# Softmax denominators as three bfloat16 parts, spread back by one bfloat16 matmul two steps later

## The chip, the cores and the metric

The kernel runs on one core of one Trainium2 chip, as one program. The core has a matrix engine (PE, whose weight loads the profile keeps apart as PEld), a vector engine (DVE), a scalar engine (ACT), GpSimd (POOL) and a sync engine (SP) that issues most of the transfers. Each engine takes its instructions in the order in which they were written; engines wait for one another and for transfers by semaphores. The metric is the time of one execution on the device in microseconds, lower is better.

## The reference

A post-norm transformer layer on 8 sequences of 1024 tokens, width 256, in float32. Only the attention matters here:

```
scores = einsum('bhid,bhjd->bhij', q, k) * scale + gated_bias
attn   = softmax(scores, axis=-1)
out    = einsum('bhij,bhjd->bhid', attn, v)         # 16 heads of 16
x      = layernorm(x + out @ Wo.T + bo)
x      = layernorm(x + moe(x))                      # 8 experts, top 2, with a capacity
```

The bias of a pair of positions depends on their distance and on a gate of the query. The softmax is computed as exponentials, whose sums over the keys come out of the same product as the numerators; the division by these sums is the part that is changed.

## The kernel before, in words

The attention comes first (about the first 2570 us of the trace), then the experts. The attention is cut into 64 **units**: a unit is two heads of one sequence, a **batch** of eight units is one sequence. A unit is 16 **steps** of the main loop (L1296): step s handles key block j = s // 2 and query half c = s % 2. In a step, PE makes the scores of two heads (L1093), DVE adds the gated bias near the diagonal (L1108), ACT takes the exponential (L1115), and at odd steps PE multiplies the last exponentials with the values (L1123), which are extended by a column of ones, so that rows 0 to 15 of each group of 32 in `o_acc` are numerators and row 16 is their sum. Beside this each step finds the row maxima of a unit 21 steps ahead: two half products on PE (L1009, L1013), a relu on ACT (L1038), a fold on DVE (L1050). POOL makes the gated bias `gb` for a key block four steps ahead, once in two steps (L969), and a diagonal of gates `dgb`, once in two steps (L982).

The order is written out by hand: the loop issues the instructions, each engine runs its own in that order. Around the fixed work of a step hang **streams**, Python generators that advance by what they yield: the prologue of the next batch (projections, `pq`, `pv`, `pg`, `pgt`), the epilogue of the last one (output projection `po`, norm, router: `px`, `pl`, `pc`), and sixteen scatters of its rows, which are indirect transfers that POOL issues one at an odd step (L874). They share one PSUM bank, `bank`; a stream that holds it lets no other in (L1222), and generators in `own` (`divide`, `shift`) go ahead of the rest. `after(n, f)` runs f in the n-th following call of `free`, once in a step (L1212, L443).

What is done with a unit u's sums runs in the steps of unit u+1:

- at the end of step 1 ACT copies `o_acc` to `osb` (`take_outputs`, L1132, copy L1135);
- at step 2 SP issues four transfers that spread the four rows of sums over 128 partitions, 16 numbers each (`move_sums`, L1140);
- at step 4 DVE takes the reciprocals of this 128x16 tile (L1156);
- at step 5 SP issues four transfers that bring them back as four rows of 512, `recs` (`move_back`, L1150);
- at step 8 (`DIVIDE_AT`) PE multiplies a 4x128 selector with `recs` in float32, which puts each row on its group of 32 partitions (`divide`, L1163); at step 9 DVE multiplies `osb` by it (L1167) and SP stores the four outputs into `oD` (L1177).

SP's queue in those steps also has the loads of unit u+3: `ks` at step 3, `ks_d` at step 4 (six transfers each), `qs` at step 6 (seven, L893 and L901); `bias` at step 8 (L936), `gates` at steps 9 and 15 (L951), `biasb` at step 1 (L915); the streams' stores (`gd`, `fd`, `kd`, `qd`, `dd`); zero fills once in four steps up to unit 22 (L397); and at step 13 the two stores of the next unit's shifts, `row` (L1078). These shifts are made by `shift` (L1061) from step 11 on (`SHIFT_AT`), and the scores of the next unit read them from its step 0 on. The step before step 11 lets no stream take the bank. Streams of a batch are started at step 12 of its first unit.

## Time and profile before

| | us |
|---|---|
| three runs | 3739.71, 3731.26, 3739.18; median 3739.18 |
| the profiled execution | 3731.06, of which its span 3729.3 |
| PE busy | 3300.4 (88%) |
| POOL busy | 2225.9 (60%), 1760.73 of the 2340 us from 200 to 2540, in the attention |
| ACT, DVE busy | 2039.4 (55%), 1905.9 (51%) |
| the matmul that spreads the reciprocals (L1163) | 78.8 busy, 72.4 idle before it |

Times in the profile are of this one execution. "L12" is a line of the kernel; `pb<-recs,sel` names what is written and what is read. In a timeline a row is a start, a duration, an engine, a line, an operation, and in brackets how long the engine sat idle before it and what ended that. Matmuls are pipelined: a row's duration is longer than the distance to the next row, and the distance is what a matmul costs in a row of them. The granted clock of PE (PEclk) is a share of its full rate.

### The profile page before, as it was taken

How to read it: one execution, taken by the hardware profiler on the slowest of the kernel's cores; microseconds unless marked ns; L12 is line 12 of the kernel's file. 1: busy time of each engine (PE TensorE's matmuls, PEld its weight loads, DVE VectorE, ACT ScalarE, POOL GpSimd, SP SyncE). 2: the span in 40 equal slices, each digit the busy share in tenths (PEclk: the TensorE clock that was granted, in tenths of full speed). 3: DMA queues.
4: the chain of work that ended last, by engine and by line, in shares of the span. 5: the costliest groups of instructions: out<-in, count | busy, mean ns of one | idle time of the engine just before them, and what ended most of it. 6: DMA issues, size and time to landing. Idle time of an engine off the chain costs nothing. (4 is left out here: it accounts for less than half of the span.)

```text
span 3729.3 us, 53473 instructions
## 1 busy us (share of the span) xinstructions
PE 3300.4 (88%) x16263; PEld 1659.6 (45%) x16263; DVE 1905.9 (51%) x5559; ACT 2039.4 (55%) x3084; POOL 2225.9 (60%) x2619
## 2 busy tenths in 40 slices
PE   2699899999999999999999999995199999999998
PEld 1233243333334334333433333332176667677776
DVE  2356565555665666566566565662034344344343
ACT  1377676767777777777776777772022222222222
POOL 2467566776786787787687788683333333333332
PEclk9799899999999999999999999997599999999999
DMA  4467656665553443443444434330323321233220
GB/s 107 125 186 192 174 158 179 190 188 178 170 159 112 133 134 121 149 125 121 131 138 137 136 115 138 118 111 27 106 51 89 88 87 57 90 93 95 69 90 22
DMA packets 380594, 455.71 MB, mean 122 GB/s; under 512 B 87653, under 2 KB 285410, under 8 KB 380282
## 3 DMA queue, kind: packets, MB, share of 16 engines
q1 hardware_dynamic: 338602, 388.06, 35.3%
q0 software_dynamic: 19296, 43.38, 4.0%
q10 hardware_dynamic: 22384, 20.58, 1.9%
q8 instruction: 138, 2.26, 0.2%
q14 instruction: 174, 1.43, 0.1%
HBM read 315.16 MB, written 140.54 MB: 122 GB/s over the span
## 5 line engine op out<-in xcount | busy, mean ns | idle before, releaser
L1115 ACT ACTIVATE pr<-sc 128x1024 f32<-128x1024 f32 x1024 | 1046.2, 1022 | 296.3 <-DVE sc L1108 291.9
L1050 DVE CUSTOM_DVE_ANT_0 over<-pm,over 128x512 f32<-128x512 f32 x1024 | 704.0, 687 | 906.8 <-ACT over L1038 335.9
L969 POOL TENSOR_TENSOR gb<-bias,gates 128x1024 f32<-128x1024 f32 (+2 forms) x512 | 1071.1, 2092 | 144.9 <-DMA gates<-gd 67.0
L1038 ACT ACTIVATE over<-pm 128x512 f32<-128x512 f32 x1024 | 609.3, 595 | 357.1 <-PE pm L1013 344.3
L1093 PE MATMUL sc<-qs,ks 122*128 122x512 bf16 x2048 | 622.6, 385 | 25.9 <-ACT pr L1115 16.9
L1108 DVE TENSOR_TENSOR sc<-sc,gb 128x640 f32<-128x640 f32 (+3 forms) x768 | 599.9, 781 | 58.5 <-POOL gb L969 34.4
L1013 PE MATMUL pm<-biasb,dgb 128*128 128x320 bf16 (+2 forms) x2048 | 580.8, 284 | 17.4 <-POOL dgb L982 17.0
L1123 PE MATMUL o_acc<-pr,v 128*17 128x512 f32 x4096 | 556.9, 616 | 0.3 <-ACT pr L1115 0.3
L1458 PE MATMUL ph<-xsT,w 128*128 128x512 f32 (+1 forms) x1440 | 488.0, 497 | 13.0 <-ACT xsT L1398 13.0
L1473 PE MATMUL py<-w,hT 128*128 128x256 f32 x2208 | 485.0, 379 | 5.3 <-DVE ys L1480 5.3
L1473 PEld LDWEIGHTS py<-w,hT 128*128 128x128 f32 x2208 | 419.2, 190 | 74.0 <-issue 10.3
L1009 PE MATMUL pm<-ks,qs 120*128 120x512 bf16 x1024 | 397.8, 388 | 40.0 <-DVE mh L1050 13.8
L1009 PE MATMUL pm<-ks_d,qs 120*128 120x512 bf16 x1024 | 395.6, 386 | 31.3 <-ACT over L1038 22.4
L1009 PEld LDWEIGHTS <-qs 120*128 120x128 bf16 x2048 | 208.4, 102 | 462.4 <-issue 296.2
L1465 ACT ACTIVATE hT<-ph,b_sb 128x512 f32<-128x512 f32 (+1 forms) x360 | 211.6, 588 | 287.7 <-PE ph L1458 287.7
L1458 PEld LDWEIGHTS ph<-xsT,w 128*128 128x128 f32 x1440 | 270.4, 190 | 212.9 <-issue 167.0
L1398 ACT COPY xsT<-pt 128x512 f32<-128x512 f32 (+1 forms) x90 | 39.5, 489 | 567.1 <-PE pt L1395 567.1
L1013 PEld LDWEIGHTS <-dgb 128*128 128x128 bf16 x2048 | 201.9, 99 | 304.0 <-issue 174.0
L143 POOL TENSOR_TENSOR rs<-rstd,neghalf 128x1 f32<-128x1 f32 x138 | 78.6, 570 | 427.3 <-DVE rstd L141 426.6
L982 POOL TENSOR_TENSOR dgb<-anti,grev 128x256 bf16<-128x256 f32 x512 | 315.0, 616 | 5.0
L1093 PEld LDWEIGHTS <-ks 122*128 122x128 bf16 x2048 | 198.0, 100 | 210.1 <-issue 64.1
L1493 POOL DMA_INDIRECT out_dram<-o,dst_i x138 | 145.6, 1055 | 168.7 <-DVE o L145 65.8
(184 smaller groups left out, 2837.7 us busy)
## 6 DMA issues: line engine op xcount, KB each, us to landing
gates<-gd SPq DMA_DIRECT2D x64, 832.0 KB
biasb<-stripb SPq DMA_DIRECT2D x128, 288.0 KB
gates<-gd SPq DMA_DIRECT2D x64, 576.0 KB
bias<-blocks SPq DMA_DIRECT2D x64, 512.0 KB
xd<-zero SPq DMA_DIRECT2D x51, 522.0 KB
ks<-kd SPq DMA_DIRECT2D x384, 64.0 KB
qs<-qd SPq DMA_DIRECT2D x384, 64.0 KB
yd<-zero SPq DMA_DIRECT2D x40, 512.0 KB
```

The source lines that it names most:

```text
L969: nc.gpsimd.tensor_tensor(gb_[:, :, off : off + hi - lo], me.bias[:, :, off : off + hi - lo], gates[:, :, lo - at : hi - at], ALU.mult,)
L982: nc.gpsimd.tensor_tensor(dg, anti.unsqueeze(1).to_broadcast([P, HP, P]), batches[b].grev[:, i, hp * HP : (hp + 1) * HP] .unsqueeze(2) .to ...
L1009: nc.tensor.matmul(pm, QS[u % 3][:R_SHIFT, h, i * P : (i + 1) * P], keys, start=True, stop=False)
L1013: nc.tensor.matmul(pm[:, lo:hi, :], dgb[m - h][:, h, :], me.biasb[:, at : at + (hi - lo) * P].rearrange("p (j n) -> p j n", n=P)[:, :, :HALF],
L1038: nc.scalar.activation(me.over, pm, AF.Relu)
L1050: nc.vector.tensor_tensor_reduce(out=me.over, in0=me.rest, in1=me.over, scale=1.0, scalar=-3.0e38, op0=ALU.add, op1=ALU.max, accum_out=me. ...
L1093: nc.tensor.matmul(me.sc[:, h, :], ks[:, h, j * P : (j + 1) * P], qs[:, h, c * CH : (c + 1) * CH], start=True, stop=True,)
L1108: nc.vector.tensor_tensor(sc[:, :, lo - c * CH : hi - c * CH], sc[:, :, lo - c * CH : hi - c * CH], me.gb[j][:, :, off : off + hi - lo], A ...
L1115: nc.scalar.activation(pr, sc, AF.Exp)
L1123: nc.tensor.matmul(o_acc[r : r + D + 1, :], batches[b].v[:, j, hp * HP + h, :], prs[c][:, h, :], start=(j == 0), stop=(j == NI - 1),)
L1458: nc.tensor.matmul(ph[:, :size], w1_sb[:, k, f * P : (f + 1) * P], xsT[:, k, :size], start=(k == 0), stop=(k == NK - 1),)
L1473: nc.tensor.matmul(py, hT[:, f, t * P : (t + 1) * P], w2_sb[:, f, :], start=(f == 0), stop=(f == NF - 1),)
```

## The change

The three cuts are made on the spread tile, after the reciprocal: POOL copies the remaining value to bfloat16 and subtracts the copy, so that three bfloat16 numbers add up to the float32 one. `move_back` brings three times four rows, `recs` is 12 rows of 512 in bfloat16, and the selector is 12x128 in bfloat16, one matmul that also adds the three parts. The cut is at step 5, `move_back` at step 6, the `qs` load at step 7 in place of 6, `divide` at step 10 in place of 8, and the streams of a batch start at step 14 of its first unit in place of 12.

```diff
-DIVIDE_AT = 8
+DIVIDE_AT = 10
...
-        sel = cst.tile([4, 4, 32], F32, name="sel")
+        sel = cst.tile([12, 4, 32], BF16, name="sel")
         nc.gpsimd.memset(sel, 0.0)
-        nc.gpsimd.affine_select(
-            out=sel, in_=sel, compare_op=ALU.not_equal, fill=1.0, base=0,
-            pattern=[[-1, 4], [0, 32]], channel_multiplier=1,
-        )
+        for a in range(3):
+            nc.gpsimd.affine_select(
+                out=sel, in_=sel, compare_op=ALU.not_equal, fill=1.0, base=-4 * a,
+                pattern=[[-1, 4], [0, 32]], channel_multiplier=1,
+            )
...
+            def cut():
+                rest = me.sums
+                me.rp = rt.tile([P, 3, 4 * CH // P], BF16, tag="rp", name=f"rp{u}")
+                for a in range(3):
+                    nc.gpsimd.tensor_copy(me.rp[:, a, :], rest)
+                    if a < 2:
+                        nc.gpsimd.tensor_tensor(
+                            rest, rest, me.rp[:, a, :], ALU.subtract
+                        )
             def move_back():
-                me.recs = rt.tile([4, CH], F32, tag="recs", name=f"recs{u}")
+                me.recs = rt.tile([12, CH], BF16, tag="recs", name=f"recs{u}")
                 for r in range(4):
-                    nc.sync.dma_start(
-                        out=me.recs[r : r + 1, :].rearrange("o (p n) -> o p n", p=32),
-                        in_=me.sums[r * 32 : (r + 1) * 32, :],
-                    )
+                    for a in range(3):
+                        nc.sync.dma_start(
+                            out=me.recs[a * 4 + r : a * 4 + r + 1, :].rearrange(
+                                "o (p n) -> o p n", p=32
+                            ),
+                            in_=me.rp[r * 32 : (r + 1) * 32, a, :],
+                        )
             after(1, move_sums)
             after(3, lambda: nc.vector.reciprocal(me.sums, me.sums))
-            after(4, move_back)
+            after(4, cut)
+            after(5, move_back)
...
-                if sb == 12:
+                if sb == 14:
...
-                    for which, at_ in enumerate((3, 4, 6)):
+                    for which, at_ in enumerate((3, 4, 7)):
```

## The prediction

> **What bounds the kernel now.** I read the page's slices first: the attention is the stretch to 2570 us; there PE shows 9 tenths nearly throughout, POOL 6 to 8. Then the waits, most of all those of the changed matmul.
>
> ```profile
> PE   2699899999999999999999999995199999999998
> POOL 2467566776786787787687788683333333333332
> PEclk9799899999999999999999999997599999999999
> ...
> PE pb L1163 <- DMA recs<-sums: 65.7, 25, 8.3
> DVE sc L1108 <- POOL gb L969: 34.4, 34, 2.6
> ```
>
> PE sets the pace, and in 25 of 64 units it stands still until the reciprocals have come back. I call "round i" the time between the copy of unit i's `o_acc` (L1135) and the next one. The timelines of SP and PE in round 53, which begins at 2221.71, show why it waits:
>
> ```profile
> 2222.34 2.45 SPq L1140 DMA_DIRECT2D sums<-osb  x4
> 2224.88 2.85 SPq L901 DMA_DIRECT2D ks<-kd  x6
> 2227.78 2.75 SPq L901 DMA_DIRECT2D ks_d<-dd  x6
> 2230.63 2.90 SPq L1150 DMA_DIRECT2D recs<-sums  x4
> ...
> 2233.15 0.27 PE L1013 MATMUL pm<-biasb,dgb 128*128 128x256 bf16 x1
> 2234.81 1.09 PE L1163 MATMUL pb<-recs,sel 4*128 4x512 f32 x2 [1.39 <-DMA recs<-sums]
> 2235.84 0.39 PE L1009 MATMUL pm<-ks,qs 120*128 120x512 bf16 x1
> 2236.06 0.27 PE L1013 MATMUL pm<-biasb,dgb 128*128 128x256 bf16 x1
> ...
> 2237.17 1.91 PE L1123 MATMUL o_acc<-pr,v 128*17 128x512 f32 x8
> ```
>
> SP is busy without a gap from 0.63 to 11.8 us of the round; PE starts 1.28 us after its last `recs` issue (13.10 against 11.82). The issues of SP are the path, at 0.61 us each (the usual four in 2.44). And a wait costs more than itself: the values product at 2237.17 takes 1.91 us, elsewhere 1.05. The windows around it have the clock (after PEld, DVE, ACT, POOL comes PEclk):
>
> ```profile
> 2232.00:2236.00 4.00, 2.61 (x13) 0.91 (x10) 1.18 (x3) 2.69 (x4) 3.74 (x10) 1.00 0.19 58
> 2236.00:2240.00 4.00, 4.00 (x17) 0.98 (x16) 2.37 (x7) 1.62 (x2) 2.30 (x8) 0.60 0.72 216
> 2240.00:2244.00 4.00, 4.00 (x25) 1.61 (x24) 2.99 (x7) 2.76 (x4) 3.47 (x9) 0.98 0.44 163
> ```
>
> After 1.39 us of waiting the clock is 0.60 for 4 us. Of 20 waits of over 1.2 us in the rounds at places 4 to 7 of a batch, 19 are followed by such a slow product; scores to the next step's L1009 take 4.13 there for 2.61. I count 1.2 us a wait.
>
> POOL is the second thing to see, in round 30 (from 1354.07), where it also issues scatters:
>
> ```profile
> 1363.10 2.38 POOL L969 TENSOR_TENSOR gb<-bias,gates 128x1024 f32<-128x1024 f32 x1
> 1365.41 0.63 POOL L982 TENSOR_TENSOR dgb<-anti,grev 128x256 bf16<-128x256 f32 x1
> 1366.21 1.01 POOL L874 DMA_INDIRECT xd<-xt,slot_i  x1 [0.17 <-issue]
> 1367.25 2.36 POOL L969 TENSOR_TENSOR gb<-bias,gates 128x1024 f32<-128x1024 f32 x1
> 1369.54 0.33 POOL L929 MEMSET biasb<- 64x256 bf16 x1
> ...
> 1367.06 1.09 PE L1163 MATMUL pb<-recs,sel 4*128 4x512 f32 x2 [2.29 <-DMA recs<-sums]
> ```
>
> The memset is step 7's, so the `dgb` before it is step 5's: POOL reaches step 5 at 12.0 us of the round, PE had reached step 8 at 10.7. A pair of steps costs POOL 4.14 us with a scatter, PE 3.6. This lag is in all rounds at places 6 and 7 of batches 1 to 6 (10.0 to 15.9 us), nowhere else in the light rounds (4.0 to 7.3).
>
> **The change part by part.**
>
> *The matmul.* From its start to the next product it takes 1.03 us (2234.81 to 2235.84); a bf16 product over 512 columns steps in 0.22 (2235.84 to 2236.06). Saved 0.81 x 64 = 52 us, all on PE's path.
>
> *Eight more issues and two steps.* `recs` takes 12 x 0.61 = 7.3 us of SP. No trace has 32-byte pieces; bounds per issue are SP's cheapest here (0.42, `bias`) and 0.68, what `recs` costs between zero fills; I take 0.61, the same 32 pieces. The `qs` load stays behind `recs`, so it neither helps nor hurts. In round 53 the issues would run from 8.92 to 16.2, and land at 17.5. Step 8 was ready at 11.7; step 10 is two steps later, 15.3. So the wait is 2.2 instead of 1.4: the two steps buy 3.6 us, the issues cost 4.9.
> - Place 5: +0.75 each, in six batches +5.
> - Place 4: no wait in rounds 28, 36, 52. Walking the streams' yields with starts two steps later, `dd` and `qd` come to lie ahead of `recs` there (+1.1), landing 18.7 against 12.75 + 3.6 + 0.5 for one more count: 1.8 and 1.2 for the clock. Four batches +12, two with zero fills +5.
> - Batch 0: four waits of 4.8 instead of 3.55: +5.
> - Places 0, 2, 3: step 10 comes at 20 to 25 us, landing at 18 to 21: nothing. If streams were lighter there it would be 1 to 2 each.
>
> *The cut on POOL.* Five small operations. The nearest rows, 128x8 (0.19 to 0.21, 0.28 apart when dependent), give 1.3 us; at most 5 x 0.32 (128x64). Where POOL keeps up this lies beside SP's loads: in round 53 it would run from 6.0 to 7.3, SP comes at 8.9. Behind it on POOL wait the scatter and step 6's `gb`, needed four steps later. But at places 6 and 7 POOL is late, and now SP stands at `recs` behind it, with `qs`, `bias` and `gates` in the queue. Round 30: cut 12.0 to 13.3, issues to 20.6, landed 21.9, while step 10 was due at 14.3: a wait of 7.6. POOL works on through it and its next step 5, at 48.5 from the same start, becomes 49: cut to 50.4, landing 59.0, while PE, from 21.9 on, is there after 16 steps, the transpose and the clock (30.8), at 52.7: 6.3 more. Then 20.1 to the end of round 31, with `po` twice: 79.1 for the two rounds, where rounds 14/15, 22/23, ... 54/55 took 72.7, 69.0, 69.0, 72.3, 69.3, 70.1, mean 70.4. Without the saving already counted that is +10.3, six times: +62. Bounds: nothing, if POOL's catching up pays for it all, and +13, if the later wait is as the first.
>
> *The `row` store.* At place 1 of batches 0 to 6 SP has 18 `gd`/`fd` stores and no gap; `row` ends at 30.1 to 31.0 in rounds 25 to 49, lands 2.1 later (round 17), and the next scores start at 33.9. After: +4.9 for issues, +0.5 since POOL's cut ends at 10.3, -1.6 as `kd` and `dd` fall behind `row`: landing 36.5. PE has one projection less before it (-1.5): 32.4. A wait of 4.1 and 1.2: six rounds (round 1 has 5 us to spare) +30. Bounds: 0, if SP's stretch breaks up, and +50.
>
> *End.* In round 63 nothing covers the chain: sums, reciprocal, cut 1.3, eight issues 4.9: +6.3. Rounds 58 to 62 by the same sums: +9. The selector's two more selects, 0.3 each, lie in the setup beside loads; at worst +0.6. The stream's bank slot moves from step 10 to 8, as many as before; nothing.
>
> Sum: -52 +5 +17 +5 +62 +30 +15 = +82. Against the profiled 3731.06 that is 3813; the median of the runs is 8 higher, I add half of it: 3817.
>
> The Trainium skill, "TensorE: Matmul & The Clock Gate", section "Why this matters for your kernels", asks for no idle gaps of PE above about 3 us. The row above has the clock down after 1.39 us, so the measurement decides; by the rule the waits of 1.8 to 2.2 us would cost no clock, and the sum would be about 7 less (six waits of place 4 at 1.2). "DMA: Bandwidth & Descriptors", "Rules for kernel authors", says to gather many small transfers into a large one, as below 64 KB one pays mostly overhead; that speaks against twelve transfers of 1 KB in place of four of 2 KB, and the rows agree: 0.61 us an issue whatever it carries.
>
> **Rivals.**
> - *SP late, POOL not* (0.20): PE's stall in the first round of a pair is time that POOL owed anyway (DVE waits for `gb` there, 34.4 us in all). The +62 go, half of the 30 with the looser queue: 82 - 62 - 15 = +5 to +25, 3740 to 3765. Against it: those 34.4 us are all it could give back.
> - *Hidden, faster* (0.08): if an issue of 32-byte pieces took under 0.42 us, round 53's twelve would land by 15.2, in time for 15.3. Then 52 us are saved, and most of the 57 us of waits before the last round with some 20 clock drops: -50 to -100, 3640 to 3690. Against it: none of the 512 issues of such shape took less than 0.50.
> - *The matmul stays dear* (0.02): if three parts cost as much as two float32 passes, +52 on the sum, 3869. Every bf16 row speaks against it.
> - *The queue breaks down* (0.03): `row` late in more rounds, 3880 to 3920.
> - *They cancel* (0.05): within 0.3% of before, 11 us, which is about what this kernel's runs tell from nothing.
>
> **How the numbers follow.** The forecast (0.62) with the bounds of pair, row and issue gives 3775 to 3875. The range goes from 3746, which takes in most of the first rival, to 3875. Faster 0.08; same 0.09, with a fifth of the first rival; slower 0.83.
>
> **What would show it.** `pb` as one bf16 matmul x64 of about 0.4 us. `recs` x768, at about 0.6. PE's waits for `recs` well above 65.7 us, in over 30 units, the longest but the last at places 6 and 7, with SP idle before L1150 until POOL. More slices of PEclk below 9. PE's waits for `row` above 17 us. Wrong I would be if `recs` were issued faster, or if the lag of POOL at step 5 vanished with the streams' new places.

## The result and the profile after

The kernel after takes 3938.12 us in the median of four runs (3923.87 to 3943.97) and the kernel before 3739.09 (3731.26 to 3739.71). The ratio is 1.0531, with an interval of 1.0502 to 1.056: 199 us slower. The forecast was 78 us slower with a range up to 3875. The direction was right and the size was not.

The profiled execution of after has 3943.97 us, its span 3942.2. The experts take as long as before (2842.6 to 3942.2, before 2631.7 to 3729.3). What was added lies in the attention, from the first copy of `o_acc` on. These are the slices of the page (the span in 40 equal parts, tenths busy; PEclk is the granted clock):

```profile
PE   2678798878888988988998988887359999999998
...
POOL 2457566776776786787688677677223333333332
PEclk9889899989989989998998998889579999999999
```

PE had nines nearly throughout the attention; now most of its slices have an eight or less. PEclk is below nine in eleven slices before the end of the attention, where it was in two. POOL is not fuller per slice. PE stands still more often. The waits (engine, what it wanted to run, what ended the wait, then us in total, times, longest) say for what:

```profile
PE pb L1180 <- DMA recs<-rp: 134.8, 28, 13.8
...
PE pc L809 <- POOL incl L739: 79.0, 43, 7.7
PE pm L1011 <- DMA qs<-qd: 78.4, 35, 6.7
...
PE sc L1095 <- DMA qs<-row: 25.7, 7, 6.9
...
PE pm L1011 <- DVE mh L1052: 13.3, 35, 1.3
```

These are the same of the kernel before:

```profile
PE pc L807 <- POOL incl L737: 31.3, 17, 7.7
...
PE sc L1093 <- DMA qs<-row: 7.6, 4, 4.1
...
PE pm L1009 <- DMA qs<-qd: 5.0, 1, 5.0
```

The first has doubled (65.7 before, in 25 units). The third is new in the rounds: the one wait of 5.0 us before lies at 115 us, ahead of the first round, and after has one of 6.7 there and 34 in the rounds. It is the start of the row maxima of unit u+2 (u is the unit whose steps run), which reads the `qs` that SP has just loaded. The second is the epilogue's count of places. The loads of `gates` stand in the same queue: POOL waited 267.2 us for them, before 67.0, but DVE's wait for the `gb` that POOL makes from them is 29.1, before 34.4, so PE did not stand for that. Round 45, which begins at 2064.22, shows the new wait. First SP's queue, then PE:

```profile
2070.30 2.75 SPq L903 DMA_DIRECT2D ks_d<-dd  x6
2073.15 7.51 SPq L1164 DMA_DIRECT2D recs<-rp  x12
2080.70 0.55 SPq L895 DMA_DIRECT2D qs<-fd  x1
2081.30 2.85 SPq L903 DMA_DIRECT2D qs<-qd  x6
```

```profile
2081.87 0.37 PE L1180 MATMUL pb<-recs,sel 12*128 12x512 bf16 x1 [0.95 <-DVE sc L1110]
...
2086.05 0.61 PE L1011 MATMUL pm<-ks_d,qs 120*128 120x512 bf16 x1 [2.97 <-DMA qs<-qd]
...
2086.75 1.91 PE L1125 MATMUL o_acc<-pr,v 128*17 128x512 f32 x8
```

The twelve issues take 7.51 us. `recs` is there in time for `pb`, which is now one short bf16 matmul. But `qs` could be issued only behind it: its last issue ends at 2084.15, and PE, at step 11, waits 2.97 us until it has landed. The values product behind the wait takes 1.91 us and not 1.05. The windows (after PE, PEld, DVE, ACT and POOL comes PEclk) show the clock under it:

```profile
2078.00:2082.00 4.00, 3.05 (x19) 0.91 (x17) 2.79 (x9) 3.86 (x6) 3.84 (x9) 1.00 0.06 9
...
2086.00:2090.00 4.00, 3.95 (x15) 1.01 (x16) 0.31 (x1) 1.78 (x3) 1.52 (x3) 0.50 0.88 324
```

Of the values products of eight matmuls, 44 are now more than 0.3 us over the median of 1.05 (22 before), by 36.7 us together (17.0 before). These are called slow products below.

### The profile page after: what moved, and what is told of

Its sections match the earlier page's. It is cut to its first block, busy times and chain, and to the rows that moved or that the text cites. A ratio compares the mean times of both kernels' runs of the same rounds, so it can differ in the third digit from the quotient of the medians.

```text
span 3942.2 us, 54539 instructions
## 1 busy us (share of the span) xinstructions
PE 3317.5 (84%) x16199; PEld 1656.4 (42%) x16199; DVE 1909.4 (48%) x5559; ACT 2045.0 (52%) x3084; POOL 2285.4 (58%) x2941
## 3 DMA queue, kind: packets, MB, share of 16 engines
q8 instruction: 138, 2.26, 0.2%
## 5 line engine op out<-in xcount | busy, mean ns | idle before, releaser
L971 POOL TENSOR_TENSOR gb<-bias,gates 128x1024 f32<-128x1024 f32 (+2 forms) x512 | 1069.7, 2089 | 367.3 <-DMA gates<-gd 267.2
L1095 PE MATMUL sc<-qs,ks 122*128 122x512 bf16 x2048 | 640.7, 395 | 38.3 <-DMA qs<-row 25.7
L1015 PE MATMUL pm<-biasb,dgb 128*128 128x320 bf16 (+2 forms) x2048 | 590.2, 288 | 16.6 <-POOL dgb L984 16.6
L1125 PE MATMUL o_acc<-pr,v 128*17 128x512 f32 x4096 | 577.4, 636 | 0.3 <-ACT pr L1117 0.3
L1011 PE MATMUL pm<-ks_d,qs 120*128 120x512 bf16 x1024 | 404.2, 395 | 95.4 <-DMA qs<-qd 78.4
L1011 PE MATMUL pm<-ks,qs 120*128 120x512 bf16 x1024 | 410.3, 401 | 36.5 <-DVE mh L1052 13.3
```

The lines of the kernel that those rows point to most:

```text
L971: nc.gpsimd.tensor_tensor(gb_[:, :, off : off + hi - lo], me.bias[:, :, off : off + hi - lo], gates[:, :, lo - at : hi - at], ALU.mult,)
L1011: nc.tensor.matmul(pm, QS[u % 3][:R_SHIFT, h, i * P : (i + 1) * P], keys, start=True, stop=False)
L1015: nc.tensor.matmul(pm[:, lo:hi, :], dgb[m - h][:, h, :], me.biasb[:, at : at + (hi - lo) * P].rearrange("p (j n) -> p j n", n=P)[:, :, :HALF],
L1095: nc.tensor.matmul(me.sc[:, h, :], ks[:, h, j * P : (j + 1) * P], qs[:, h, c * CH : (c + 1) * CH], start=True, stop=True,)
L1125: nc.tensor.matmul(o_acc[r : r + D + 1, :], batches[b].v[:, j, hp * HP + h, :], prs[c][:, h, :], start=(j == 0), stop=(j == NI - 1),)
```

## The experiments

The theory after the result ("SP"): SP issues in order, `qs` stands behind `recs`, and the eight additional issues push it past step 11, where unit u+2's row maxima begin; the matmul's gain is real. The rivals: "POOL", the cut on POOL is what costs, by its time or by holding SP; and "places", the later divide and the later streams cost by themselves. The 95% interval is in brackets behind each ratio to the kernel before. 1% is 37.5 us. As before, place p means the rounds i with i mod 8 = p, here without round 62; sums over a place compare profiled executions. That of before has 3731.06 us, and the medians of before beside the experiments are 3746 to 3752, so, if that is spread evenly over the places, up to 2.6 us of such a sum is not the edit's.

**Eight more issues, and nothing else.** The kernel before, with

```diff
             def move_back():
...
+                spare = rt.tile([8, 32, 8], F32, tag="spare", name=f"spare{u}", bufs=1)
+                for r in range(8):
+                    nc.sync.dma_start(
+                        out=spare[r : r + 1, :, :],
+                        in_=me.sums[r % 4 * 32 : (r % 4 + 1) * 32, :8],
+                    )
```

> The kernel before, with eight more transfers of 32 pieces of 32 bytes issued by SP right behind recs, into a tile that nothing reads; matmul, divide step and cut are as before. Theory SP (SP's issues are in order, and eight more of them put the qs load past step 11, where unit u+2's row maxima begin): recs itself is as early as before, so the wait for recs stays near 65.7 us in 25 rounds, but qs lands 4.9 us later, about 21.4 us into a light round where step 11 is reached at 19.5; a wait for qs of about 1.9 us and 1.2 for the clock in some 30 rounds is 93, and about 4 for the row store in seven rounds is 28: near 3860, and the wait at pm for qs goes from 5.0 us to 50 or more. Theory POOL (the cut on POOL and the epilogue's later place on POOL are what costs): without them only the row store is late, 3740 to 3770. Theory places (the later divide and streams cost by themselves): 3740 to 3770 as well.

1.0429 [1.0406, 1.0451], 161 us more than before. The waits of this kernel:

```profile
PE pm L1009 <- DMA qs<-qd: 111.9, 38, 6.4
...
PE pb L1169 <- DMA recs<-sums: 63.9, 25, 8.3
...
PE sc L1093 <- DMA qs<-row: 27.4, 10, 5.2
```

The wait for `recs` is what it was (65.7), that for `qs` goes from 5.0 to 111.9, that for `row` from 7.6 to 27.4. Slow products go from 22 to 39. Round 37 of this kernel (from 1726.70) shows all of it, SP's issues and PE's two waits:

```profile
1735.63 2.54 SPq L1150 DMA_DIRECT2D recs<-sums  x4
1738.22 5.02 SPq L1156 DMA_DIRECT2D spare<-sums  x8
1743.29 0.55 SPq L893 DMA_DIRECT2D qs<-fd  x1
1743.88 2.67 SPq L901 DMA_DIRECT2D qs<-qd  x6
```

```profile
1739.46 1.09 PE L1169 MATMUL pb<-recs,sel 4*128 4x512 f32 x2 [1.05 <-DMA recs<-sums]
...
1748.89 0.58 PE L1009 MATMUL pm<-ks_d,qs 120*128 120x512 bf16 x1 [3.96 <-DMA qs<-qd]
```

`pb` waits 1.05 us (1.27 in the kernel before); nine us later the row maxima start after a wait of 3.96 for `qs`. Issues that nobody reads cost 161 us, 50 more than the theory gave: its 1.9 us a wait was too small (111.9 in 38 is 2.9).

**The moved places alone.** The kernel before, with

```diff
-DIVIDE_AT = 8
+DIVIDE_AT = 10
-            after(4, move_back)
+            after(5, move_back)
-                if sb == 12:
+                if sb == 14:
-                    for which, at_ in enumerate((3, 4, 6)):
+                    for which, at_ in enumerate((3, 4, 7)):
```

> The kernel before with the four moved places alone: divide at step 10, move_back at step 6, qs at step 7, the batch's streams from step 14. The matmul stays float32 with four transfers, and there is no cut. Theory SP: recs lands at 12.8 us of a light round and step 10 comes at 15.3, so of the 65.7 us at pb only the last round's 8 stay, with some 20 clock drops of 1.2: -80; qs is as early as before. 3655 to 3690. Theory POOL: the epilogue's later place brings back part, with PE's wait for incl at pc as in the changed kernel (79.0 us, before 31.3): 3690 to 3720. Theory places: that wait and the others take the whole gain, 3740 or more.

1.0013 [0.9994, 1.0033]. The wait for `recs` did fall, from 65.7 to 11.6 us, and none of it became time. By rounds of the profiled executions, places 5 and 6 are 25 us shorter in all, place 4 is 28 us longer and places 2 and 3 are 21 longer. These are the waits that took its place:

```profile
DVE sc L1108 <- POOL gb L969: 73.7, 49, 5.4
...
PE pc L807 <- POOL incl L737: 61.4, 35, 7.7
...
PE pm L1009 <- DMA qs<-qd: 21.6, 13, 6.8
```

They were 34.4, 31.3 and 5.0. So at place 7, where POOL is late (round 31 takes 37.5 us, before 35.7, with a wait of 3.80 for ACT in place of that for `recs`), PE's wait was time that POOL needed anyway, and the epilogue's counts at place 4 pay for the later streams. "Places" is right in that the move costs what it brings, and wrong in that it would explain the 199 us.

**Three parts in one transfer a row.** The kernel after, with `recs` as 4x32x3x16 and

```diff
-                    for a in range(3):
-                        nc.sync.dma_start(
-                            out=me.recs[a * 4 + r : a * 4 + r + 1, :]...
-                            in_=me.rp[r * 32 : (r + 1) * 32, a, :],
-                        )
+                    nc.sync.dma_start(
+                        out=me.recs[r : r + 1, :, :, :].rearrange("o p a n -> o p (a n)"),
+                        in_=me.rp[r * 32 : (r + 1) * 32, :, :].rearrange("p a n -> p (a n)"),
+                    )
...
+            for a in range(3):
+                nc.tensor.matmul(
+                    pb, sel.rearrange("p h m -> p (h m)"), me.recs[:, :, a, :],
+                    start=(a == 0), stop=(a == 2),
+                )
```

> The changed kernel, but the three parts of a row go in one transfer of 32 pieces of 96 bytes, so recs has four issues and not twelve; recs lies as four rows with the parts side by side, and pb is three accumulated bf16 matmuls of four rows in place of one of twelve (about 0.44 us more a unit, 28 in all). Cut on POOL and all places as in the changed kernel. Theory SP: the qs wait (78.4) goes and recs is in time except where POOL is late at places 6 and 7 and in the last round; against before -24 for the matmul, -60 for recs, -24 for the clock, +30 for the epilogue's wait for incl, +15 for POOL at places 6 and 7: 3660 to 3710. Theory POOL: most of the loss stays, over 3850. Theory places: 3800 or more.

1.0144 [1.0116, 1.0173], 3808.84 us: 145 less than after, though its matmul is dearer, but 100 over what "SP" gave. What was left was large, and its rounds say where: against the moved places alone, places 6 and 7 are 47 us longer (37.8 and 40.4 us in rounds 30 and 31; 31.2 and 37.5 with the moves alone), all others about as long or shorter.

**One part, at the old places.** The kernel before, with

```diff
-                me.recs = rt.tile([4, CH], F32, tag="recs", name=f"recs{u}")
+                me.recs = rt.tile([4, CH], BF16, tag="recs", name=f"recs{u}")
...
+            def turn():
+                me.rp = rt.tile([P, 4 * CH // P], BF16, tag="rp", name=f"rp{u}")
...
+                    nc.vector.reciprocal(me.rp, me.sums)
```

> The kernel before with recs in bfloat16, written so by DVE's reciprocal: the second and third parts are left out, so the reciprocals have eight bits. Four transfers of 32 pieces of 32 bytes, one bf16 matmul, all at the old places, no cut on POOL. What the matmul alone gives: 0.81 x 64 = 52 us less, 3680 to 3695, under all theories; if the wait for recs or something behind pb takes the gain, 3725 or more. The issues of 32-byte pieces at 0.61 us as those of 64 bytes; if they are cheaper, the wait of 65.7 us at pb is shorter.

0.9887 [0.9865, 0.9909], 43 us less. The bf16 matmul's gain is there when nothing else changes, somewhat under the 52 that a product's distance gave; the wait for `recs` is 60.2.

**The cut on DVE.** The kernel after, with

```diff
-                    nc.gpsimd.tensor_copy(me.rp[:, a, :], rest)
+                    nc.vector.tensor_copy(me.rp[:, a, :], rest)
                     if a < 2:
-                        nc.gpsimd.tensor_tensor(
+                        nc.vector.tensor_tensor(
```

> The changed kernel with the five operations of the cut on DVE in place of POOL, in the same step. So far: moved places alone +5 us, one part of bf16 at the old places -43, eight more issues alone +161, the changed kernel with four transfers in place of twelve +54 against before; what is left for the cut on POOL is about 5 - 24 + x = 54, so x = 73, of which places 6 and 7 of the batches hold 47 (37 and 40 us for the two rounds in place of 34 and 37 with the moved places alone). Theory both (issues and POOL each cost, and add up): 73 less than the changed kernel, a ratio of 1.030 to 1.040 to before; at places 6 and 7 SP no longer stands before recs, and PE's wait for incl at pc falls from 79.0 us to about 61 as with the moved places. Theory SP alone: under 10 us less, 1.050, since twelve issues keep PE waiting wherever the cut is made.

1.0563 [1.0535, 1.0592]: no gain at all. PE's wait for `recs` fell from 134.8 to 42.6 and that for the fold of the row maxima rose from 13.3 to 86.9. The cause is in DVE's own rows, here round 30 (from 1456.01):

```profile
1462.90 0.17 DVE L1154 CAST rp<-sums 128x16 bf16<-128x16 f32 x1
1463.11 0.17 DVE L1156 TENSOR_TENSOR sums<-sums,rp 128x16 f32<-128x16 f32 x1
1463.32 3.12 DVE L1154 CAST rp<-sums 128x16 bf16<-128x16 f32 x1
```

and in POOL's at the same time:

```profile
1462.99 1.01 POOL L876 DMA_INDIRECT xd<-xt,slot_i  x1 [0.17 <-issue]
1464.03 2.37 POOL L971 TENSOR_TENSOR gb<-bias,gates 128x1024 f32<-128x1024 f32 x1
```

The same cast of 16 numbers takes 0.17 us or 3.12: the long one ends at 1466.44, 0.04 after POOL's `gb` ends at 1466.40. Of the 320 operations of the cut 63 took over 1 us, and 51 of these end within 0.2 us of the end of a `gb`. So here a copy on DVE stood still while POOL worked on SBUF, and PE stood behind the fold behind it. What SP's shorter wait for POOL gave was paid back there.

**`ks_d` earlier.** The kernel after, with

```diff
-                    for which, at_ in enumerate((3, 4, 7)):
+                    for which, at_ in enumerate((3, 0, 7)):
```

> The changed kernel with one load moved: the six ks_d transfers of unit u+2 are issued at step 0 of unit u in place of step 4. Their buffer is free since step 11 of the unit before, and SP stands idle there in light rounds. Everything in the queue behind comes 2.75 us earlier: recs and qs. Theory qs (the deadline at step 11 is what the eight issues cost): in a light round qs lands at about 19.5 and PE is there at 20 or later, so the wait at pm for qs (78.4) falls under 25 and that for recs (134.8) to about 80, where POOL's cut is the later of the two; with 1.2 for the clock on some 30 rounds: 90 to 130 less than the changed kernel, a ratio of 1.018 to 1.030. Theory POOL alone: SP stands before recs until the cut is done, so only what is behind it in light rounds gains: under 40 less, 1.043 or more.

1.0367 [1.034, 1.0394], 61 us less than after, between what the two theories gave. The wait for `qs` fell only to 67.3: where `recs` came earlier PE did too, and `qs` still stood behind twelve issues; at places 6 and 7 and in round 28 SP stood at `recs` for POOL as before (round 28: `recs` issued from 11.2 to 18.7 us in both).

**All loads ahead, in the kernel before.** Only

```diff
-                    for which, at_ in enumerate((3, 4, 6)):
+                    for which, at_ in enumerate((1, 0, 3)):
```

> The kernel before with SP's order changed and nothing else: ks_d is loaded at step 0, ks at step 1 and qs at step 3, in place of 4, 3 and 6, so that recs stands behind sums and qs alone, and no load has to hurry behind it. If SP's issues alone made the wait of 65.7 us at pb, it falls to the last round's 8 and the clock gains 20 x 1.2: 3660 to 3680, 0.977 to 0.982. If POOL is the limit at places 6 and 7, as the moved places alone showed (the wait at pb gone there, 3.8 us for ACT behind DVE and gb in its place), 30 of it are given back there: 3690 to 3715.

0.9808 [0.9776, 0.984], 3672.08 us. Its buffers were free all along (`ks_d`'s since step 11 of the unit before, the other two once the last scores of unit u-1 have read theirs). The time is 74 us under before, in the range that the first theory gave. The wait for `recs` is 13.9 us, slow products are down to 7, and place 7 has gained nothing, as with the moves alone.

**Three transfers of 128 pieces.** The kernel after, with

```diff
-                for r in range(4):
-                    for a in range(3):
-                        nc.sync.dma_start(...)
+                for a in range(3):
+                    nc.sync.dma_start(
+                        out=me.recs[a * 4 : a * 4 + 4, :].rearrange("r (p n) -> r p n", p=32),
+                        in_=me.rp[:, a, :],
+                    )
```

> The changed kernel, but each part goes in one transfer of 128 pieces of 32 bytes: recs has three issues in place of twelve, the same 384 pieces, and pb stays one matmul of twelve rows. If an issue has its price whatever it carries (0.61 us in the rows of recs), SP is as in the run with four transfers and the matmul is 28 us cheaper: 1.005 to 1.012. If SP or the transfer pays by the piece (128 pieces 2.4 us to issue, or landing much later than 1.3 us after the issue), it stays near the changed kernel: 1.035 or more.

1.0079 [1.0053, 1.0106], 3779.61 us: 170 us less than after by one change in how the same 384 pieces are asked for. An issue costs the same with 128 pieces as with 32 (these are issues of `recs` in ns: least, median, most), after and this kernel:

```profile
L1164 SPq DMA_DIRECT2D recs<-rp x768: 502/588/1722, 212.3 to 2764.3; - x192
```

```profile
L1163 SPq DMA_DIRECT2D recs<-rp x192: 546/608/1272, 215.0 to 2609.6; - x192
```

**Loads ahead, twelve issues kept.** The kernel after, with

```diff
-                    for which, at_ in enumerate((3, 4, 7)):
+                    for which, at_ in enumerate((1, 0, 3)):
```

> The changed kernel, twelve issues and the cut on POOL kept, with SP's order changed alone: ks_d at step 0, ks at step 1, qs at step 3, so that no load stands behind recs. Theory qs (the twelve issues cost most because qs stands behind them): the wait at pm for qs (78.4 us, 67.3 with ks_d alone moved) goes to under 10, and its clock with it; the waits for recs stay where POOL is late (places 6 and 7) and become 0 to 1.5 elsewhere: recs ends at 15 to 16 in a light round, lands 1.3 later, and step 10 comes at 15.3. 120 to 150 less than the changed kernel, 1.013 to 1.022. Theory POOL: SP is kept standing at recs by the cut as before and the waits for recs grow by what those for qs lose; 1.035 or more.

1.0166 [1.014, 1.0191], 137 us less than after, as "qs" said. The wait for `qs` is 4.9 us, once, that for `recs` 90.1 in 20. The eight issues, the cut and the moved places are all there, only the loads no longer stand behind them, and two thirds of the loss are gone. Not all of that is `qs`: PE's wait for it fell by 73.5 us and that for `recs` by 44.7, and the same order gave the kernel before 74 us. With the loads ahead in both kernels the change still costs 134 us. The rounds of places 6 and 7 are still 40 us over before in all.

**The streams' start back.** The kernel with three transfers, and

```diff
-                if sb == 14:
+                if sb == 12:
```

> The run with three transfers, with one number back: the batch's streams start at step 12 of its first unit as in the kernel before, and not at step 14. If the later start is what costs at place 4 (28 us over the eight batches with the moved places alone, by PE's wait for incl at pc, 2.7 to 4.0 us in the round, and two more counts in it), place 4 gets them back and PE's wait for incl falls from 75 us to about 35: 1.008 less 0.008, 0.997 to 1.003. If that wait comes from the cut on POOL, it stays, and the ratio stays at 1.006 to 1.010.

1.0034 [1.0022, 1.0047], 17 us less. Place 4 went from 26 us over before to 6 over and place 3 from 9 over to 19 under, but PE's wait for `incl` fell only from 75.0 to 55.3, and places 1 and 7 lost 21 us of it. The ratio lies just above what was expected.

**All of it together.** The kernel after, with three transfers, loads ahead (steps 1, 0 and 3), streams at step 12, divide at step 9, `move_back` at step 5, and

```diff
+            def turn():
+                me.rp = rt.tile([P, 3, 4 * CH // P], BF16, tag="rp", name=f"rp{u}")
+                me.rest = rt.tile([P, 4 * CH // P], F32, tag="rest", name=f"rest{u}")
+                nc.vector.reciprocal(me.rest, me.sums)
+                nc.vector.tensor_copy(me.rp[:, 0, :], me.rest)
+
             def cut():
+                eng = nc.gpsimd
+                eng.tensor_tensor(me.rest, me.rest, me.rp[:, 0, :], ALU.subtract)
+                eng.tensor_copy(me.rp[:, 1, :], me.rest)
+                eng.tensor_tensor(me.rp[:, 2, :], me.rest, me.rp[:, 1, :], ALU.subtract)
```

> A version from what the runs showed: the three bf16 parts and one matmul of the changed kernel, in three transfers of 128 pieces, with the loads ahead (ks_d, ks, qs at steps 0, 1, 3), the streams at step 12 as before, divide at step 9, move_back at step 5. DVE writes the reciprocal and its first part, POOL makes the rest in three operations in place of five (0.8 us). Against the kernel before with the loads ahead (0.981): the matmul gives 43 to 52; recs goes out at about 9 in a light round, lands at 12.5 and step 9 comes at 13.5, so no wait there; POOL, which sets the pace at places 6 and 7, has 0.8 us more in each of 14 rounds, 11 us, and SP holds qs no longer. 3625 to 3650, 0.968 to 0.975. If POOL's lag holds recs at places 6 and 7 by 4 us as with three transfers, 50 more: 0.982 or above, no better than the loads alone.

0.9803 [0.9779, 0.9827], 3677.79 us: no better than the loads alone, whose interval it shares. Places 1, 2, 3 and 6 gained 33 us in all against the loads alone, and place 4 lost 36; and PE's wait for the fold rose from 24.3 to 46.7. DVE's one copy is held by POOL here too (ns: least, median, most):

```profile
L1153 DVE CAST rp<-rest x64: 174/592/4597, 210.1 to 2492.2; 128x16 bf16<-128x16 f32 x64
```

**The cut on DVE in two places of eight.** The same, with

```diff
             def cut():
-                eng = nc.gpsimd
+                eng = nc.vector if (u + 1) % UB >= 6 else nc.gpsimd
                 eng.tensor_tensor(me.rest, me.rest, me.rp[:, 0, :], ALU.subtract)
...
```

> The same, but at places 6 and 7 the three operations of the cut are on DVE. POOL is then free of the cut where it is late. The cut on DVE made PE wait 1.6 us a round for the row maxima's fold (86.9 us in all where DVE made all five operations in every unit): 14 rounds of 1 us or less are 14, and POOL's part of 11 and its lag are gone. If POOL's lag holds recs in the version with POOL throughout, this one is 20 to 50 us faster than that; if it does not, within 5 us of it.

0.9879 [0.9858, 0.99], 29 us slower. The expectation names places 6 and 7, and the line of code chose 5 and 6; it tells nothing of place 7. At places 5 and 6, where it did act, the rounds are 8 and 25 us longer in all. PE hardly waited for `recs` there in the version it was to mend (1.8 us, once), and 42 of DVE's 112 copies and subtractions of the cut took over 1 us.

**The cut alone.** The kernel before, with the five operations on POOL at step 5, into a tile that nothing reads:

```diff
+            def cut():
+                rp = rt.tile([P, 3, 4 * CH // P], BF16, tag="rp", name=f"rp{u}")
+                rest = rt.tile([P, 4 * CH // P], F32, tag="rest", name=f"rest{u}")
+                nc.gpsimd.tensor_copy(rp[:, 0, :], me.sums)
+                nc.gpsimd.tensor_tensor(rest, me.sums, rp[:, 0, :], ALU.subtract)
...
+            after(4, cut)
```

> The kernel before, with the five operations of the cut on POOL at step 5, made into a tile that nothing reads. Recs, matmul, issues and places are as before, so SP stands behind nothing new: what is left is POOL's own 1.3 us a unit. Theory POOL's time: at places 6 and 7 POOL sets the pace, 14 rounds x 1.3 = 18 us, and little elsewhere; 1.004 to 1.007. Theory held queue (the cut costs because SP stands at recs until POOL is done, with qs behind): within 6 us of before, 0.999 to 1.002.

1.0016 [0.9997, 1.0034], 6 us, in an interval that takes in nothing. This is POOL's time with no transfer waiting for it.

**The cut with SP behind it.** The kernel after in three transfers, with the places of before:

```diff
-DIVIDE_AT = 10
+DIVIDE_AT = 8
-            after(5, move_back)
+            after(4, move_back)
-                if sb == 14:
+                if sb == 12:
-                    for which, at_ in enumerate((3, 4, 7)):
+                    for which, at_ in enumerate((3, 4, 6)):
```

> The changed kernel in three transfers, with all four places as in the kernel before: divide at step 8, move_back at step 5, qs at step 6, streams from step 12. The cut on POOL (five operations) and the one bf16 matmul stay. Theory held queue: in light rounds the cut is done at 7 to 8 us and recs goes out at 9 as before, at places 6 and 7 POOL comes at 12 and holds recs and qs, as with the later places; step 8 being earlier by 3.6 us, the wait for recs there is about 5 and PE's time at places 6 and 7 is as long as in the changed kernel with three transfers (+39 us over the rounds); place 4 is as before, less the matmul. -45 + 39 + 25 for the waits at step 8: 1.003 to 1.010. Theory places: without the moved places nothing is left but the matmul's gain and POOL's 18 us, 0.990 to 0.995.

1.0044 [1.0028, 1.0061], 17 us over before and 59 over the one part at the same places (which has four issues and no cut). Set beside the cut alone, round 30 of both shows the difference: POOL, SP and PE here (the round begins at 1355.16),

```profile
1365.01 2.35 POOL L971 TENSOR_TENSOR gb<-bias,gates 128x1024 f32<-128x1024 f32 x1
...
1367.88 0.19 POOL L1154 CAST rp<-sums 128x16 bf16<-128x16 f32 x1
...
1368.10 1.99 SPq L1163 DMA_DIRECT2D recs<-rp  x3
1370.14 0.49 SPq L895 DMA_DIRECT2D qs<-fd  x1
...
1371.60 0.58 PE L1177 MATMUL pb<-recs,sel 12*128 12x512 bf16 x1 [5.35 <-DMA recs<-rp]
```

and with the cut alone (from 1353.93):

```profile
1363.09 2.44 SPq L1159 DMA_DIRECT2D recs<-sums  x4
...
1366.39 0.19 POOL L1150 CAST rp<-sums 128x16 bf16<-128x16 f32 x1
...
1366.86 1.09 PE L1173 MATMUL pb<-recs,sel 4*128 4x512 f32 x2 [2.09 <-DMA recs<-sums]
```

POOL comes to the cut 12.5 to 12.7 us into the round in both. Where `recs` needs the cut, SP stands until then with `qs` behind, and PE waits 5.35 us; where it does not, SP has issued at 9.2 us and PE waits 2.09. Places 6 and 7 are 47 us over before here, 14 with the cut alone, and 2 under with the one part. So "held queue" stands for the cut.

**Divide at step 8.** The version with all of it together, with

```diff
-DIVIDE_AT = 9
+DIVIDE_AT = 8
```

> The version with all loads ahead, three transfers and three operations on POOL, with divide at step 8 in place of 9, as in the kernel before. Recs is landed by 10.4 to 12.1 us in the light rounds but those of place 7, and step 8 comes at 11.7. If divide's later place is what shifts the epilogue's counts (place 4 took 22 us more than before with divide at step 9, and 14 less with the loads alone ahead, divide at 8), place 4 is 15 to 20 us under before again: about 36 us less than with divide at 9, 0.969 to 0.973. If the cut on POOL makes it (the count waits for POOL's rp there), place 4 stays and the ratio stays at 0.978 to 0.983.

0.9879 [0.9863, 0.9896]. Half of the expectation came true: place 4 went from 22 over before to 10 under. But places 6 and 7 went from 27 under to 18 over, since `recs` there comes after step 8 (PE waits 3.04 us in round 31), and the whole is 28 us slower.

**One transfer for the sums.** The same, with

```diff
-                for r in range(4):
-                    nc.sync.dma_start(
-                        out=me.sums[r * 32 : (r + 1) * 32, :],
...
+                nc.sync.dma_start(
+                    out=me.sums,
+                    in_=me.osb.rearrange("(r q) n -> r q n", q=32)[:, D, :].rearrange(
+                        "r (p n) -> r p n", p=32
+                    ),
+                )
```

> The same as that with divide at 8, and the four rows of sums go to the 128 partitions in one transfer of 128 pieces in place of four of 32. SP saves 1.8 us between the copy of o_acc and the reciprocals, and as much in the last round: 2 us there and less than 10 elsewhere, 0 to 0.003 less than with four, if nothing waits for recs any more; 20 us or more if recs is still late at places 6 and 7.

0.9861 [0.9834, 0.9887], in an interval that overlaps with that of the version it changes: the three issues saved ahead of the reciprocals have no price that these runs can show. PE's waits moved all the same, that for `recs` from 32.4 to 55.5 us and that for the fold from 54.9 to 39.4.

**Divide at step 8, at places 6 and 7 at step 9.** The version with divide at step 8 and four transfers for the sums, with

```diff
-            if u and s == DIVIDE_AT:
+            if u and s == DIVIDE_AT + (u % UB in (0, 7)):
```

> The version with all loads ahead and divide at step 8, but at places 6 and 7 divide is at step 9. If place 4's loss belongs to the shift of the epilogue's counts and that of places 6 and 7 to recs after step 8 alone, both are undone: about 45 us less at places 6 and 7 than with step 8 throughout, 3660 on a before of 3750, 0.974 to 0.979. If POOL's lag carries the loss on whatever the step, 0.983 or more.

0.9852 [0.9826, 0.9877]. Place 4 stays at 12 under, place 6 gets 17 of its loss back, place 7 none. The ratio falls into the second of the two ranges: the loss at these places is only in part that of the step. What else sets place 7 is open.

**The first part on POOL as well, at places 0 to 5.** The same, with

```diff
             def turn():
...
-                nc.vector.tensor_copy(me.rp[:, 0, :], me.rest)
+                if u % UB >= 6:
+                    nc.vector.tensor_copy(me.rp[:, 0, :], me.rest)
...
             def cut():
+                if u % UB < 6:
+                    eng.tensor_copy(me.rp[:, 0, :], me.rest)
```

> The same, with the first part's copy on POOL (four operations there) at places 0 to 5 and on DVE at 6 and 7. If DVE's extra copy of 0.2 us behind the reciprocal delays the fold that PE waits for (46.7 to 54.9 us at pm, 24.3 without it), the wait falls to about 30 and the time by 10 to 25 us: 0.969 to 0.975. If the fold is late for another reason, within 5 us of the other.

0.9848 [0.9821, 0.9875], the same time. PE's wait for the fold goes from 46.1 to 42.0 and no further, though only 16 copies are left on DVE. DVE's copy is not the main cause of it in this version.

## Why the prediction was wrong

**The step that failed** is the sentence "The `qs` load stays behind `recs`, so it neither helps nor hurts." The prediction followed `qs` as a thing that could delay `recs` and never asked when `qs` itself was due. It is due at step 11: row maxima run 21 steps ahead, so unit u+2's begin there. Its slack could be read in the kernel before, in round 53:

```profile
2234.17 2.67 SPq L901 DMA_DIRECT2D qs<-qd  x6
...
2241.46 0.38 PE L1009 MATMUL pm<-ks_d,qs 120*128 120x512 bf16 x1
```

The last issue ends at 2236.84 and step 11's product starts 4.6 us later. Less the 1.90 us that the landing took in round 45 of after, some 2.7 us are to spare, by this estimate, and eight issues take 4.9. Behind twelve issues `qs` is late in 34 rounds. Eight issues that delay nothing but what stands behind `recs` cost 161 us, and three issues in place of the twelve give 170 back. In the prediction's own sum the issues had some 65 beside the pairs of places 6 and 7: `row`, place 4, place 5, batch 0 and part of the end.

**What the forecast left out, in PE's waits.** From before to after PE waits 73 us more for `qs` and 48 more for `incl`, which had both been given nothing: 121 us, and the result is 121 us above the forecast. Waits replace one another and slow the clock, so that the two agree so closely is in part luck. The waits for `recs` and `row`, which the forecast did count, grew by 69 and 18.

**The matmul**, -52: right in kind (64 matmuls, 0.37 us each), measured at -43 by the one part. In round 45 the next product starts 0.30 us after `pb` (2081.87 to 2082.17), where 0.22 had been taken.

**Place 4**, +17: the rounds are 45 us longer over the eight batches (round 28: 39.4 against 32.0), and in round 28 not for `recs`, which is in time. The step that failed here is "The stream's bank slot moves from step 10 to 8, as many as before; nothing." In round 28 PE waits 3.97 us for `incl` at one count, 0.92 before. With the moves alone the round takes 38.9, waiting 2.74 us there; with three transfers, the streams started at 12 again take place 4 from 26 over to 6.

**Places 6 and 7**, +62, a pair of rounds 79.1 for 70.4: the six pairs of after are 85.7, 84.0, 80.3, 79.7, 78.2 and 79.5, mean 81.2. Its mechanism, SP standing at `recs` behind a late POOL, is shown by the cut alone (6 us) against the same cut with SP behind (59), but in after it is only a part. In round 30 POOL comes to the cut 10.5 us into the round and not at 12.0; the wait for `recs` is 5.66 and not 7.6, and 1.61 for `qs` comes on top. Over these twelve rounds SP stands idle before `recs` for 23 us in all, and not at all in rounds 46, 47 and 54, whose pairs are long all the same: there SP's own issues make `recs` late. That the sum came out near is luck. With three transfers in place of twelve the two places are 39 over before, and with twelve 70: cut and issues both have their part there.

**Batch 0**, +5: four waits of 4.5 to 5.0 us for `recs`, where 4.8 had been worked out.

**Place 5**, +5: measured 31. In round 53 PE waits 2.55 us for `recs`, where 2.2 had been worked out, and then 2.2 more at step 11.

**`row`**, +30: place 1 is 32 us longer, a right size for a wrong reason in four of six rounds. Rounds 9 and 17 wait for `row`, 1.4 and 3.1 us longer than before, and round 1, which was given 5 us to spare, 6.9; rounds 25 to 49 do not wait for it at all and wait 1.84 to 2.71 for `qs` instead. Places 0, 2 and 3, given nothing, are 4, 17 and 2 longer although the matmul saves 5 in each; in place 2 it is `row` in batches 0 to 2 (2.26, 3.50 and 2.09 us) and `qs` in round 2 (2.77).

**The end**, +6.3: the last wait for `recs` is 13.8 for 8.3.

**The rivals.** "SP late, POOL not" was right in one thing: part of PE's stall at places 6 and 7 is time that POOL owed anyway, for the moves alone shortened the two places by 8 us in all and place 7 not at all. "Hidden, faster" needed an issue under 0.42 us; the median is 0.588. "The queue breaks down" came nearest, with 3880 to 3920 for 3938, and named `row`; `row` grew by 18 us of waits and `qs` by 73.

**The clock.** Of the 34 waits for `qs` in the rounds of after, 32, of 1.38 to 3.38 us, are followed by a product of 1.91 us in place of 1.05; the two others are of 0.97 and 1.93. So waits well under 3 us cost clock here, as the prediction read from its row. The product alone is 0.86 us of its 1.2 a wait; the rest was not measured apart.

**The rule on small transfers.** The prediction cited the Trainium skill, "DMA: Bandwidth & Descriptors", "Rules for kernel authors", for gathering small transfers. The runs agree, and more strongly than the prediction used it: the same bytes in three transfers in place of twelve are 170 us. Its 0.61 us an issue held for the pieces of `recs`: in the median 0.588 with 32 of 64 bytes (before) or of 32 (after).

## What to carry to other kernels

In an in-order queue, write down for everything behind an insertion when it is due, not only what it delays; what is wanted soonest goes first, and loads whose buffers are free early are asked for early. The order of three loads was worth more here (1.9%) than the cheaper matmul with one part (1.1%), and the order with all three parts was worth no more than the order alone. And a transfer that gathers what several did costs one issue: look for a shape that lets one transfer span all partitions before counting issues as given.

## What the runs showed of the hardware

SP's price of a transfer between SBUF tiles goes by the issue: 0.588 us in the median with 32 pieces of 32 bytes, 0.608 with 128. The landing is not much later: in round 30 `pb` starts 1.37 us after the last of twelve issues of 32 pieces (after), and 1.52 after the last of three of 128 (the cut with SP behind it).

A small DVE copy can take some twenty times its time beside POOL: 0.17 us alone, up to 3.12 with the cut on DVE and 4.60 with all of it together, where all 31 copies of over 1 us end within 0.2 us of the end of a `gb`, a product of two SBUF tiles. The same happened to subtractions of two SBUF tiles (17 of 128 over 1 us). DVE's reciprocals, with one input, (L1156 and its like, 64 in each kernel) took 0.23 to 0.26 us in every kernel of this study, also where they wrote bfloat16, and also where they started while a `gb` ran: 26 of 64 with all of it together, where the 34 copies that started so took 1.95 us in the median. The Trainium skill, "SBUF — State Buffer", "Who interferes with whom", says that copies and casts can enter fast modes that take a port pair which DVE shares with GpSimd, that the one that issues first holds it for its whole instruction, that a DVE operation with two SBUF inputs contends with a GpSimd instruction that reads SBUF, and that one with at most one SBUF input outside those modes does not. These rows agree. A version whose first part is written by a second reciprocal, and not by a copy, follows from it and wasn't tried.

What stays open: the version with all of it together and the loads alone end at the same time, so the matmul's 43 us are lost again, at place 4 with divide at step 9, at places 6 and 7 with divide at step 8, and in part in the wait for the fold (46.7 for 24.3). No order of this study has both. One part with the loads ahead was not run, so how much of the loss is the cut's is not shown.
